# Two encoder layers on one core: grouped heads' output weights summed by accumulating transfers, and the second sequence's rows loaded as squares for VectorE to transpose

## The chip, the cores and the metric

The kernel runs on one core of a Trainium2 chip. Its engines work beside each other, each on its own queue of instructions: TensorE (PE, with its weight loads as PEld), VectorE (DVE), ScalarE (ACT), GpSimd (POOL) and SyncE (SP), which here only issues transfers. Sixteen DMA engines move the data. The metric is the device time of one execution in microseconds. Before the change it is 481.82 us, the median of three runs (481.68 to 482.26).

## The reference, cut to what matters

Two layers, each an attention and a feed-forward part, each followed by a sum with its input and a layer norm. Only the first attention and the first feed-forward part meet the change. x has 2 sequences of 512 rows of 512 numbers; all is float32.

```python
q = (x @ Wq.T + bq).reshape(b, s, 32, 128)
sig_q = elu(q) + 1
q_sel = sig_q[:, :, ::4, :]                      # 8 heads are used
num = einsum('bshd,hde->bshe', q_sel, M)
den = einsum('bshd,hd->bsh', q_sel, z)[..., None] + 1e-6
out_heads = repeat(num / den, 4, axis=2)         # each result serves 4 heads
x = layernorm(x + out_heads.reshape(b, s, 4096) @ Wo.T)
# feed-forward: gate and up products, values truncated to integers, down product
x = layernorm(x + ffn(x))
```

Since each of the eight results is repeated for a group of four heads, the four blocks of Wo that belong to a group can be summed first: the result times the sum of the blocks is the same as the sum of the four products.

## The kernel before, in words

**Order.** One function writes the whole program for all engines. A scheduler of the framework orders the instructions of TensorE, VectorE and ScalarE, by priorities and a model of times; GpSimd's order is as written, and SyncE's transfers go out in the order of the program. `tc.issue_after` ties an instruction behind another. Pools of tiles set what waits for what: a tile with a tag gets the next buffer of that tag, and its first writer waits until the readers of the buffer's earlier tile are done. All PSUM tiles come from one pool of eight (`ps`, line 66).

**First attention.** `load_x(0)` (line 74) loads the four row blocks of sequence 0, SyncE and ScalarE in turn. `transposed` (line 106) turns row blocks into `xt`, with the 512 columns on partitions in four groups `k`: 16 TensorE transposes into PSUM, then four copies, two by ScalarE and two by VectorE (line 119). `queries(b, xt, h)` (line 328) makes head `h`: four matmuls of 128x512, ScalarE's `e` and `r` (lines 340 and 342), VectorE's `q` (line 344). The first loop over the heads (line 432) works on sequence 0, the second (line 442) on sequence 1. After head 4 of sequence 0, `turn_memory` (line 347) transposes the eight blocks of M. After head 6, `transposed(xs[1], "a01")` (line 439) transposes sequence 1, whose rows were loaded behind wq (line 295).

**Output weights.** For each head, two transfers (line 306) bring the four blocks of Wo as two tiles of two blocks. `sum_weights` (line 355) adds them with two instructions, one of 128x1024 and one of 128x512, four heads on VectorE and four on GpSimd. `fold(h)` (line 363) multiplies the sum by M's block on TensorE, and ScalarE puts the product, less its last column, into `mw` (lines 367 and 368); the last column of `mw` is z, copied there by GpSimd (line 326). The folds stand behind heads 0, 2, 3, 5 and 6 of sequence 1.

**Checks.** Beside this, ScalarE and VectorE check whether the gate and up weights are ternary: `largest` over chunk 0 (line 450), `scales` (line 455), and from head 3 of sequence 1 three `check_up` (line 417) for each head. Their weights `gu` come by SyncE behind the blocks of Wo (line 310), then the small weights of the second layer (lines 312 to 320).

**Reading.** `read(b, t, between)` (line 370) runs eight matmuls `po` for each of eight row blocks; ScalarE and VectorE divide and add them to x, GpSimd adds the first three heads' part (lines 396 and 405).

**End of the first feed-forward part.** `f0_down(i)` (line 625) runs the down product of row block `i` (11 matmuls into `pd`), ScalarE scales it (`scaled`, line 610), block `i - 1` is truncated and subtracted from x with its statistics taken (`added`, line 616), and block `i - 2` is normalised (line 635), tied behind the statistics of the block after it. Before the last block's product, line 677 calls `transposed(xs[0], "a10")`, which the second layer's attention (`pqk`, line 778) needs.

Of the kernel before, what the change touches and what calls it, by code (L numbers as in the profile page):

```python
# [10 lines left out]
F32 = mybir.dt.float32  # L11
# [8 lines left out]
P = 128  # L20
# [7 lines left out]
LN_EPS = 1e-5  # L28
DEN_EPS = 1e-6
LAST = HID - 1  # L30
LENT = 3
TOP12 = -4096
BELOW_HALF = 0.5 - 2.0**-13
# [3 lines left out]
def kernel(  # L37
# [36 lines left out]
    def load_x(b):  # L74
        for t in range(NT):
            x = xp.tile([P, HID], F32, tag="x", name=f"x_{b}_{t}")
            eng = nc.scalar if b == 0 and t % 2 else nc.sync
            eng.dma_start(x, x_in[b, ts(t, P), :])
            xs[b].append(x)

    load_x(0)
    bq = const.tile([D, NH], F32, tag="bq", name="bq")
    z = const.tile([D, NH], F32, tag="z", name="z")

    ident = const.tile([P, P], F32, tag="ident", name="ident")
    make_identity(nc, ident)
    ln_eps = const.tile([P, 1], F32, tag="ln_eps", name="ln_eps")
# [4 lines left out]
    nc.vector.memset(den_eps, DEN_EPS)  # L92
    below_half = const.tile([P, 1], F32, tag="below_half", name="below_half")
    nc.vector.memset(below_half, -BELOW_HALF)
    ones = const.tile([P, P], F32, tag="ones", name="ones")
    nc.vector.memset(ones, 1.0)


    rise = psum("rise")
# [52 lines left out]
    def layernorm_apply(out, row, stats):  # L152
        mv, rstd = stats
        nc.vector.tensor_scalar(
            out, row, mv[:, 0:1], rstd, ALU.subtract, ALU.mult
        )
# [119 lines left out]
    def pair_tile(name):  # L276
        return wop.tile([P, 2, HID], F32, tag="wo", name=name)
# [6 lines left out]
    with tc.tile_pool(name="a0w", bufs=1) as a0w, tc.tile_pool(name="a0", bufs=2) as a0:  # L284
        wq = []
        for h in range(NH):
            if h % 2 == 0:
                two = query_tile(f"wq{h}").rearrange("p a (k d) -> p a k d", k=NK)
            w = two[:, h % 2]
            nc.sync.dma_start(w, wq_in[h])  # L290
            wq.append(w)
            if h == 0:
                nc.sync.dma_start(bq, bq_in)
                nc.sync.dma_start(z, z_in)
        load_x(1)
        m = a0w.tile([D, NH, D], F32, tag="m", name="m")
        nc.sync.dma_start(m, m_in)

        wos = []
        for h in range(NH):  # L300
            halves = []
            if h == 6:
                gus = up_weights(gu0_in, "0", range(1))
            for j in range(2):
                w = pair_tile(f"wo{h}_{j}")
                nc.sync.dma_start(w, wo0_in[h, :, ts(j, G // 2), :])
                halves.append(w)
            wos.append(halves)

        gus += up_weights(gu0_in, "0", range(1, len(CHUNKS)))  # L310
        wqkv = const.tile([P, NK, 3 * D], F32, tag="wqkv", name="wqkv")
        nc.sync.dma_start(wqkv, wqkv_in.rearrange("(k p) f -> p k f", p=P))
        bqk = const.tile([D, 3], F32, tag="bqk", name="bqk")
        nc.sync.dma_start(bqk, bqk_in)
        bv = const.tile([P, D], F32, tag="bv", name="bv")
        nc.sync.dma_start(bv, bv_in.to_broadcast([P, D]))
        wo1 = const.tile([D, HID], F32, tag="wo1", name="wo1")
        nc.sync.dma_start(wo1, wo1_in)
        bo = const.tile([P, HID], F32, tag="bo", name="bo")
        nc.sync.dma_start(bo, bo_in.to_broadcast([P, HID]))  # L320

        mw = a0w.tile([D, NH, HID], F32, tag="mw", name="mw")
        nc.gpsimd.tensor_copy(mw[:, :, LAST], z)

        def queries(b, xt, h, cuts=1):

# [25 lines left out]
        def sum_weights(eng, h):  # L355

            w, w1 = wos[h]
            eng.tensor_add(w, w, w1)
            s = a0.tile([D, HID], F32, tag="wos", name=f"wos{h}", bufs=4)
            eng.tensor_add(s, w[:, 0, :], w[:, 1, :])  # L360
            wos[h] = s

        def fold(h):
            p = psum(f"pmw_{h}")
            nc.tensor.matmul(p, m[:, h, :], wos[h], start=True, stop=True)
            c = small.tile([P, 1], F32, tag="col", name=f"col_{h}")
            nc.scalar.mul(c, p[:, LAST:], -1.0)
            nc.scalar.activation(mw[:, h, :LAST], p[:, :LAST], AF.Identity, bias=c)

        def read(b, t, between):  # L370

            x = xs[b][t]
            ys, steps = [], []
            for h0 in range(0, NH, 4):
                four = []
                den = small.tile([P, 4], F32, tag="den", name=f"den_{b}_{t}_{h0}")
                for j in range(4):
                    po = psum(f"po0_{b}_{t}_{h0 + j}")
                    nc.tensor.matmul(  # L379
                        po, qs[b][h0 + j][:, ts(t, P)], mw[:, h0 + j, :],  # L380
                        start=True, stop=True,
                    )
# [49 lines left out]
        for h in range(NH):  # L432
            queries(0, xt, h, 1 if h else 2)
            if h == 4:
                sum_weights(nc.gpsimd, 0)
                turn_memory()
                sum_weights(nc.vector, 1)
            elif h == 6:
                xt1 = transposed(xs[1], "a01")
                sum_weights(nc.vector, 2)  # L440
        sum_weights(nc.gpsimd, 3)
        for h in range(NH):
            queries(1, xt1, h)
            if h == 0:
                sum_weights(nc.vector, 4)
                sum_weights(nc.gpsimd, 5)
                fold(0)
                fold(1)
                mx_up = largest(
                    [gus[0][:, a].rearrange("p k i -> p (k i)") for a in range(2)], "up"  # L450
                )
            elif h == 1:
                top_up = over_partitions(mx_up, "up")
            elif h == 2:
                sc_up, inv_up = scales(top_up, "up")
                fold(2)
                fold(3)
                sum_weights(nc.vector, 6)
                sum_weights(nc.gpsimd, 7)
            elif h == 3:  # L460
                fold(4)
            elif h == 5:
                fold(5)
                fold(6)
            elif h == 6:
                fold(7)
            if h >= 3:
                for _ in range(3):
                    check_up(*checks.pop(0))
# [54 lines left out]
    with tc.tile_pool(name="f0", bufs=2) as f0:  # L524
# [88 lines left out]
            cut_to_12(y)  # L613
            ys[i] = y

        def added(i):
            b, t = order[i]
            ta, tb = truncated_parts(f0, ys[i], P, f"d{i}")

            x = xs[b][t]  # L620
            nc.vector.scalar_tensor_tensor(x, tb, 128.0, x, ALU.min, ALU.subtract)
            nc.vector.scalar_tensor_tensor(x, x, -1.0, ta, ALU.mult, ALU.add)
            stats[i] = layernorm_stats(x, f"f0_{i}")

        def f0_down(i):
            if i < len(order):
                pds[i] = down(*order[i])
                scaled(i)
            if 0 <= i - 1 < len(order):
                added(i - 1)  # L630
            if 0 <= i - 2 < len(order):

                b, t = order[i - 2]
                with tc.issue_after(taken[f"f0_{min(i, len(order)) - 1}"].ins):
                    layernorm_apply(xs[b][t], xs[b][t], stats[i - 2])

        to_divide[2:2] = [None, None]
        for c in range(3):
# [35 lines left out]
        up(1, 10, moved.values())  # L674
        for i in range(2, len(order) - 1):
            f0_down(i)
        xt_a1 = [transposed(xs[0], "a10")]
        for i in range(len(order) - 1, len(order) + 2):
            f0_down(i)

    gus = up_weights(gu1_in, "1", range(6, len(CHUNKS)))
# [487 lines left out]
```

## Time and profile before

| | |
|---|---|
| median of three runs | 481.82 us |
| the profiled execution's own time | 481.89 us |
| its span, first to last instruction | 479.7 us |
| granted TensorE clock, mean | 0.997 |
| data moved by transfers | 33.98 MB, 20.18 MB of it in the first 80 us |
| wo transfers (line 306) | 16 of 512 KB, median 7.6 us from issue to landing |
| transposes of sequence 1 (line 115) | 16, first weight load at 31.71 us |
| first fold, last fold (weight loads) | 40.33 us, 67.98 us |
| first matmul of the read stage (weight load) | 71.85 us |
| first pqk of the second layer | 239.17 us |

The span counts from the first to the last instruction of the profiled execution; some 2.2 us lie around it. In lines of the timeline the first number is the start in microseconds, the second the length; "xN" counts merged instructions, and the brackets at the end give the idle time of the engine before and what released it. float32 matmuls of 128x512 stand in the profile as two instructions, 0.43 us apart.

### The profile page before, as it was taken

The page shows a single profiled execution, that of the slowest core. Times are in us where ns is not written, and L with a number is a line of the kernel's source. Part 1 is how long each engine was busy: PE and PEld are TensorE (multiplying, and loading weights), DVE is VectorE, ACT ScalarE, POOL GpSimd, SP SyncE. Part 2 cuts the span into 40 slices and gives each one's busy share as a digit, 9 for nine tenths or more (in the row PEclk, how much of TensorE's full clock was granted, in tenths as well). Part 3 has the DMA queues.
Part 4 walks back from the last instruction along what each step waited for, and adds up shares of the span by engine and source line. Part 5 has one row for each costly group of instructions (what it writes and reads, how often), then busy time and mean ns, then how long its engine had stood idle before and what let it go on. Part 6 is the DMA issues. An engine that isn't in the chain of part 4 may idle for free.

```text
span 479.7 us, 5815 instructions
## 1 busy us (share of the span) xinstructions
PE 470.9 (98%) x1891; PEld 329.6 (69%) x1891; DVE 349.9 (73%) x689; ACT 272.5 (57%) x512; POOL 115.1 (24%) x146
## 2 busy tenths in 40 slices
PE   9999999999999999999999999999999999999995
PEld 8454444434487788787766567888788888888885
DVE  1345677677666586756979989997875778999852
ACT  3344899556666867546645834686753565434221
POOL 0344102666530392000464032000000000023211
PEclk9999999999999999999999999999999999999998
DMA  8999700000043001121390000000000000001011
GB/s 303 389 357 336 296 2 0 0 0 1 2 128 110 3 1 26 65 91 34 113 385 2 0 1 1 1 1 0 1 0 1 1 1 1 0 23 40 27 45 44
DMA packets 13748, 33.98 MB, mean 71 GB/s; under 512 B 1872, under 2 KB 2768, under 8 KB 13712
## 3 DMA queue, kind: packets, MB, share of 16 engines
q1 hardware_dynamic: 13280, 32.85, 19.0%
q10 hardware_dynamic: 432, 0.66, 0.4%
q8 instruction: 22, 0.36, 0.3%
q14 instruction: 14, 0.11, 0.1%
HBM read 31.40 MB, written 2.10 MB: 70 GB/s over the span
## 4 chain that ended last, share of the span: by engine, by line
PE 71%; ACT 7%; DVE 5%; issue 3%; POOL 1%; POOLq 0%; DVEq 0%; ACTq 0%
PE pm L977 17%; PE pg_f L539 9%; PE pc L977 9%; PE pu_f L539 9%; PE pdm L1052 7%; PE pd_f L595 4%; PE pdc L1052 4%; DVE x L401 4%; PE pqk L778 3%; PE po L379 2%; ACT y L392 2%; ACT t L411 2%; PE pv L791 1%; PE po L880 1%; PE pot L863 1%
## 5 line engine op out<-in xcount | busy, mean ns | idle before, releaser
L379 PE MATMUL po<-mw,q 128*128 128x512 f32 x128 | 57.1, 598 | 0.4 <-DVE mv_a L142 0.2
L334 PE MATMUL pq<-xt_a,wq 128*128 128x512 f32 (+1 forms) x136 | 56.4, 567 | 0.0
L148 POOL TENSOR_TENSOR rstd_f<-mv_f,ln_eps 128x1 f32<-128x1 f32 x15 | 4.7, 313 | 185.8 <-DVE mv_f L1063 132.1
L379 PEld LDWEIGHTS po<-mw,q 128*128 128x128 f32 x128 | 23.0, 189 | 32.2 <-issue 17.7
L334 PEld LDWEIGHTS pq<-xt_a,wq 128*128 128x128 f32 x136 | 25.5, 190 | 27.5 <-issue 25.5
L977 PE MATMUL pm<-r,it_early 128*128 128x512 f32 x144 | 37.8, 393 | 0.4 <-ACT r L718 0.4
L977 PE MATMUL pm<-r,ugu 128*128 128x512 f32 (+1 forms) x144 | 36.8, 393 | 0.0
L977 PEld LDWEIGHTS pm<-r,it_early 128*128 128x128 f32 x144 | 27.0, 188 | 6.7 <-ACT r L718 0.7
L401 DVE SCALAR_TENSOR_TENSOR x<-po,den,x 128x511 f32<-128x511 f32 x40 | 29.8, 745 | 1.9
L977 PEld LDWEIGHTS pm<-r,ugu 128*128 128x128 f32 (+1 forms) x144 | 26.8, 186 | 6.3
L170 ACT ACTIVATE ta_f<-y_f,below_half 128x512 int8<-128x512 f32 (+1 forms) x22 | 15.9, 722 | 24.4 <-DVE y_f L160 23.9
L988 DVE SCALAR_TENSOR_TENSOR ev_q<-pm,ev_q 128x512 f32<-128x512 f32 (+1 forms) x28 | 19.2, 687 | 14.0 <-PE pm L977 14.0
L396 POOL TENSOR_TENSOR y<-y,y 128x511 f32<-128x511 f32 x16 | 20.3, 1270 | 31.5 <-ACT y L392 30.8
L565 DVE SCALAR_TENSOR_TENSOR it_f<-tb_f,ta_f 128x512 fp32r<-128x512 int16 (+1 forms) x22 | 15.2, 690 | 16.0 <-ACT tb_f L171 15.9
L977 PE MATMUL pc<-r,ugu 128*128 128x512 f32 (+1 forms) x96 | 26.1, 394 | 0.0
L340 ACT ACTIVATE e<-pq,bq 128x512 f32<-128x512 f32 x16 | 11.1, 693 | 25.8 <-PE pq L334 25.8
L413 POOL TENSOR_SCALAR td<-wd,inv_down 128x512 fp32r<-128x512 f32 (+1 forms) x11 | 19.5, 1792 | 24.8 <-DVE inv_down L204 24.4
L539 PE MATMUL pg_f<-xh,tu 128*128 128x512 f32 (+1 forms) x88 | 25.1, 405 | 0.0
L539 PE MATMUL pu_f<-xh,tu 128*128 128x512 f32 (+1 forms) x88 | 24.0, 394 | 0.0
L539 PE MATMUL pg_f<-xl,tu 128*128 128x512 f32 (+1 forms) x88 | 23.9, 393 | 0.0
L539 PE MATMUL pu_f<-xl,tu 128*128 128x512 f32 (+1 forms) x88 | 23.9, 393 | 0.0
L987 ACT ACTIVATE ev_q<-pc 128x512 f32<-128x512 f32 (+1 forms) x28 | 16.4, 591 | 12.1 <-PE pc L977 12.1
(292 smaller groups left out, 1106.0 us busy)
## 6 DMA issues: line engine op xcount, KB each, us to landing
gu<-in_gu SPq DMA_DIRECT2D x20, 512.0 KB, 7.9
wo<-in_wo SPq DMA_DIRECT2D x16, 512.0 KB, 7.6
wd<-in_wd SPq DMA_DIRECT2D x20, 256.0 KB, 4.7
wq<-in_wq SPq DMA_DIRECT2D x8, 256.0 KB, 4.5
out<-x SPq DMA_DIRECT2D x7, 256.0 KB, 2.0
x<-in_x SPq DMA_DIRECT2D x6, 256.0 KB, 5.4
gu<-in_gu SPq DMA_DIRECT2D x2, 384.0 KB, 6.5
wqkv<-in_wqkv SPq DMA_DIRECT2D x1, 768.0 KB, 10.8
```

Of the source, the lines that this page charges most:

```text
L170: nc.scalar.activation(a[:n], y, AF.Relu, bias=below_half[:n])
L334: nc.tensor.matmul(pq[:, at], wq[h][:, k, :], xt[:, k, at], start=(k == 0), stop=(k == NK - 1),)
L379: nc.tensor.matmul(po, qs[b][h0 + j][:, ts(t, P)], mw[:, h0 + j, :], start=True, stop=True,)
L396: nc.gpsimd.tensor_add(ys[0][:, :LAST], ys[0][:, :LAST], y[:, :LAST])
L401: steps.append(nc.vector.scalar_tensor_tensor(x[:, :LAST], four[j][:, :LAST], d, x[:, :LAST], ALU.mult, ALU.add))
L413: eng.tensor_scalar(out, w, factor, None, ALU.mult)
L539: nc.tensor.matmul(pp[a][:n], t[:, a, i % NK, :n], x2[b][i], start=(i == 0), stop=(i == 2 * NK - 1),)
L595: nc.tensor.matmul(pd, inter[b][c][:n, ts(t, P)], td[c][:n].bitcast(F32R), start=(c == 0), stop=(c == last),)
L977: nc.tensor.matmul(p[:n], w, x, start=(left[id(p)] == begun[id(p)]), stop=(left[id(p)] == 1))
L987: nc.scalar.activation(ev[:n], pc, AF.Copy, scale=CROSS)
L988: nc.vector.scalar_tensor_tensor(ev[:n], pm, MAIN, ev[:n], ALU.mult, ALU.add)
L1052: nc.tensor.matmul(p[:, :w], got[j // 4][1][kind][:n, j % 4], down_parts[j][kind][:, cols], start=(j == 0 and kind == kinds[0]), stop=(j = ...
```

## The change

It has three parts.

First, the sums of Wo's blocks. `sum_weights` goes. Four tiles `wos[i]` hold a pair of heads each. SyncE loads block 0 of both heads into each (four transfers of 512 KB in pieces of 2 KB); then GpSimd issues twelve transfers with `accum_op=ALU.add`, blocks 1, 2 and 3 of each pair in turn, which add to what is in the tile. `fold` reads the tile directly. The folds move: two behind each of heads 4 to 7 of sequence 1.

Second, sequence 1's rows. They are first loaded as `x_squares`, in the buffer that later holds `mw`: 16 transfers of 64 KB, each with 32 partitions and pieces of 32 numbers (128 B), so that each 32x32 square of x lies where its transpose belongs. Four VectorE transposes of 128x512, which turn each 32x32 square in place, then give `xt1`. `mw` is taken after this (`begin_fold`), its column of z is loaded straight by SyncE, in pieces of one number, and behind it in SyncE's order come the rows of sequence 1 themselves (`load_x(1)`, needed in the read stage), chunks 1 to 10 of `gu`, and the second layer's small weights (`others`).

Third, smaller moves. The constant `ones` is set first. At the end of the first feed-forward part the last down product is issued ahead of the 16 transposes of `transposed(xs[0], "a10")`; the truncation of block 6 is tied behind ScalarE's two copies; the normalisation of the last block of a sequence is tied behind the second subtraction of the next block (`taken[n]`) in place of its statistics.

```diff
-            if h == 0:
-                nc.sync.dma_start(bq, bq_in)
-                nc.sync.dma_start(z, z_in)
-        load_x(1)
+        wos = [pair_tile(f"wo{i}") for i in range(NH // 2)]
+
+        def load_wo(eng, i, g, **how):
+            pair = wo0_in[ts(i, 2), :, g, :].rearrange("h d e -> d h e")
+            eng.dma_start(wos[i], pair, **how)
+
+        x_squares = a0w.tile([P, NK, S], F32, tag="mw", name="x_squares")
+        squares = x_in[1].rearrange("(f i) (k a j) -> k a i f j", i=SQ, k=NK, j=SQ)
         m = a0w.tile([D, NH, D], F32, tag="m", name="m")
         nc.sync.dma_start(m, m_in)
-        wos = []
-        for h in range(NH):
-            halves = []
-            if h == 6:
-                gus = up_weights(gu0_in, "0", range(1))
-            for j in range(2):
-                w = pair_tile(f"wo{h}_{j}")
-                nc.sync.dma_start(w, wo0_in[h, :, ts(j, G // 2), :])
-                halves.append(w)
-            wos.append(halves)
-        gus += up_weights(gu0_in, "0", range(1, len(CHUNKS)))
+        for k in range(NK):
+            for a in range(P // SQ):
+                nc.sync.dma_start(
+                    x_squares[ts(a, SQ), k].rearrange("i (f j) -> i f j", j=SQ),
+                    squares[k, a],
+                )
+        for i in range(NH // 2):
+            load_wo(nc.sync, i, 0)
+        for g in range(1, G):
+            for i in range(NH // 2):
+                load_wo(nc.gpsimd, i, g, accum_op=ALU.add)
+        gus = up_weights(gu0_in, "0", range(1))
...
+        def begin_fold():
+            mw = a0w.tile([D, NH, HID], F32, tag="mw", name="mw")
+
+            nc.sync.dma_start(mw[:, :, LAST], z_in)
+            mws.append(mw)
...
             elif h == 6:
-                xt1 = transposed(xs[1], "a01")
-                sum_weights(nc.vector, 2)
-        sum_weights(nc.gpsimd, 3)
+                xt1 = xtp.tile([P, NK, S], F32, tag="xt", name="xt_a01")
+                for k in range(NK):
+                    nc.vector.transpose(xt1[:, k, :], x_squares[:, k, :])
+                begin_fold()
+                load_x(1)
+                gus += up_weights(gu0_in, "0", range(1, len(CHUNKS)))
+                others()
...
+            elif h >= 4:
+                fold(2 * h - 8)
+                fold(2 * h - 7)
...
+        def normed(i):
+
+            b, t = order[i]
+            n = min(i + 1, len(order) - 1)
+
+            with tc.issue_after(taken[n if t == NT - 1 else f"f0_{n}"].ins):
+                layernorm_apply(xs[b][t], xs[b][t], stats[i])
...
+        i = len(order) - 1
+        pds[i] = down(*order[i])
+        scaled(i)
         xt_a1 = [transposed(xs[0], "a10")]
-        for i in range(len(order) - 1, len(order) + 2):
+        added(i - 1, (copies[-4], copies[-2]))
+        normed(i - 2)
+        for i in range(len(order), len(order) + 2):
             f0_down(i)
```

More of the change, by code (lines that the diff above doesn't have):

```diff
@@ L30 @@
 LAST = HID - 1
+SQ = 32
 LENT = 3
@@ L82 @@
     bq = const.tile([D, NH], F32, tag="bq", name="bq")
-    z = const.tile([D, NH], F32, tag="z", name="z")
+    ones = const.tile([P, P], F32, tag="ones", name="ones")
+    nc.vector.memset(ones, 1.0)
     ident = const.tile([P, P], F32, tag="ident", name="ident")
@@ L94 @@
     nc.vector.memset(below_half, -BELOW_HALF)
-    ones = const.tile([P, P], F32, tag="ones", name="ones")
-    nc.vector.memset(ones, 1.0)
     rise = psum("rise")
@@ L311 @@
+        for i in range(NH // 2):
[4 more added lines that the diff above has]
+        gus = up_weights(gu0_in, "0", range(1))
         wqkv = const.tile([P, NK, 3 * D], F32, tag="wqkv", name="wqkv")
-        nc.sync.dma_start(wqkv, wqkv_in.rearrange("(k p) f -> p k f", p=P))
         bqk = const.tile([D, 3], F32, tag="bqk", name="bqk")
-        nc.sync.dma_start(bqk, bqk_in)
@@ L315, with others @@
         bv = const.tile([P, D], F32, tag="bv", name="bv")
-        nc.sync.dma_start(bv, bv_in.to_broadcast([P, D]))
         wo1 = const.tile([D, HID], F32, tag="wo1", name="wo1")
-        nc.sync.dma_start(wo1, wo1_in)
         bo = const.tile([P, HID], F32, tag="bo", name="bo")
-        nc.sync.dma_start(bo, bo_in.to_broadcast([P, HID]))
-        mw = a0w.tile([D, NH, HID], F32, tag="mw", name="mw")
-        nc.gpsimd.tensor_copy(mw[:, :, LAST], z)
+        def others():
+            nc.sync.dma_start(wqkv, wqkv_in.rearrange("(k p) f -> p k f", p=P))
+            nc.sync.dma_start(bqk, bqk_in)
+            nc.sync.dma_start(bv, bv_in.to_broadcast([P, D]))
+            nc.sync.dma_start(wo1, wo1_in)
+            nc.sync.dma_start(bo, bo_in.to_broadcast([P, HID]))
@@ L328, in queries @@
+        mws = []
+        def begin_fold():
+            mw = a0w.tile([D, NH, HID], F32, tag="mw", name="mw")
+            nc.sync.dma_start(mw[:, :, LAST], z_in)
+            mws.append(mw)
         def queries(b, xt, h, cuts=1):
@@ L353, in turn_memory @@
                 nc.scalar.copy(m[:, 4 * i : 4 * i + 4, :].rearrange("d h e -> d (h e)"), pt)
[L355 to L361, printed above, removed]
         def fold(h):
             p = psum(f"pmw_{h}")
-            nc.tensor.matmul(p, m[:, h, :], wos[h], start=True, stop=True)
+            nc.tensor.matmul(p, m[:, h, :], wos[h // 2][:, h % 2, :], start=True, stop=True)
             c = small.tile([P, 1], F32, tag="col", name=f"col_{h}")
             nc.scalar.mul(c, p[:, LAST:], -1.0)
-            nc.scalar.activation(mw[:, h, :LAST], p[:, :LAST], AF.Identity, bias=c)
+            nc.scalar.activation(mws[0][:, h, :LAST], p[:, :LAST], AF.Identity, bias=c)
         def read(b, t, between):
@@ L379, in read @@
                     nc.tensor.matmul(
-                        po, qs[b][h0 + j][:, ts(t, P)], mw[:, h0 + j, :],
+                        po, qs[b][h0 + j][:, ts(t, P)], mws[0][:, h0 + j, :],
                         start=True, stop=True,
@@ L434 @@
             if h == 4:
-                sum_weights(nc.gpsimd, 0)
                 turn_memory()
-                sum_weights(nc.vector, 1)
             elif h == 6:
-                xt1 = transposed(xs[1], "a01")
-                sum_weights(nc.vector, 2)
-        sum_weights(nc.gpsimd, 3)
+                xt1 = xtp.tile([P, NK, S], F32, tag="xt", name="xt_a01")
[5 more added lines that the diff above has]
+                others()
         for h in range(NH):
@@ L444 @@
             if h == 0:
[L445 to L448, printed above, removed]
                 mx_up = largest(
@@ L455 @@
                 sc_up, inv_up = scales(top_up, "up")
[L456 to L466, printed above, removed]
+            elif h >= 4:
+                fold(2 * h - 8)
+                fold(2 * h - 7)
             if h >= 3:
@@ L614, in scaled, with added @@
             ys[i] = y
-        def added(i):
+        def added(i, behind=()):
             b, t = order[i]
-            ta, tb = truncated_parts(f0, ys[i], P, f"d{i}")
+            with ExitStack() as tied:
+                for step in behind:
+                    tied.enter_context(tc.issue_after(step.ins))
+                ta, tb = truncated_parts(f0, ys[i], P, f"d{i}")
             x = xs[b][t]
             nc.vector.scalar_tensor_tensor(x, tb, 128.0, x, ALU.min, ALU.subtract)
-            nc.vector.scalar_tensor_tensor(x, x, -1.0, ta, ALU.mult, ALU.add)
+            taken[i] = nc.vector.scalar_tensor_tensor(x, x, -1.0, ta, ALU.mult, ALU.add)
             stats[i] = layernorm_stats(x, f"f0_{i}")
@@ L631, in f0_down @@
             if 0 <= i - 2 < len(order):
-                b, t = order[i - 2]
-                with tc.issue_after(taken[f"f0_{min(i, len(order)) - 1}"].ins):
-                    layernorm_apply(xs[b][t], xs[b][t], stats[i - 2])
+                normed(i - 2)
[4 more added lines that the diff above has]
+                layernorm_apply(xs[b][t], xs[b][t], stats[i])
         to_divide[2:2] = [None, None]
@@ L676 @@
             f0_down(i)
+        i = len(order) - 1
+        pds[i] = down(*order[i])
+        scaled(i)
         xt_a1 = [transposed(xs[0], "a10")]
-        for i in range(len(order) - 1, len(order) + 2):
+        added(i - 1, (copies[-4], copies[-2]))
+        normed(i - 2)
+        for i in range(len(order), len(order) + 2):
             f0_down(i)
```

## The prediction

> **What bounds the kernel now.** I began with the page's first parts: the span, the busy shares, and the forty slices with what the DMA engines moved.
>
> ```profile
> span 479.7 us, 5815 instructions
> PE 470.9 (98%) x1891; PEld 329.6 (69%) x1891; DVE 349.9 (73%) x689; ACT 272.5 (57%) x512; POOL 115.1 (24%) x146
> PE   9999999999999999999999999999999999999995
> DMA  8999700000043001121390000000000000001011
> PE 71%; ACT 7%; DVE 5%; issue 3%; POOL 1%; POOLq 0%; DVEq 0%; ACTq 0%
> ```
>
> TensorE (PE) is busy throughout, and the chain of waits runs through it for 71% of the span. So a TensorE instruction removed is worth its spacing, and a wait put before TensorE costs its length. But the first five slices (60 us) are also full of DMA, so transfers there are not free. The view of windows gives that stage: length, then busy time of PE, PEld, DVE, ACT and POOL, granted clock, DMA share, GB/s.
>
> ```profile
> 12.00:32.00 20.00, 20.00 (x54) 9.28 (x53) 8.99 (x11) 7.43 (x13) 7.53 (x4) 1.00 1.00 368
> 32.00:53.00 21.00, 21.00 (x64) 10.17 (x63) 10.25 (x19) 10.78 (x22) 7.12 (x4) 1.00 0.95 365
> 53.00:72.00 19.00, 19.00 (x46) 8.48 (x45) 14.10 (x33) 18.45 (x36) 0.44 (x1) 1.00 0.23 80
> 72.00:131.00 59.00, 58.65 (x149) 25.10 (x147) 42.44 (x96) 39.59 (x107) 31.06 (x33) 1.00 0.00 1
> 233.00:240.00 7.00, 5.96 (x32) 4.49 (x31) 6.82 (x16) 4.85 (x9) 2.61 (x6) 1.00 0.64 202
> ```
>
> The reader is to see full DMA engines until 53 us, ACT full from 53 to 72, no transfers from 72 to 131, and a gap of TensorE at 233 to 240. Then I took the timeline of TensorE's weight loads around the second sequence's transposes and folds, and of the gap.
>
> ```profile
> 31.29 0.19 PEld L334 LDWEIGHTS pq<-xt_a,wq 128*128 128x128 f32 x1 [0.24 <-issue]
> 31.71 0.14 PEld L115 LDWEIGHTS pt_a<-ident,x 128*128 128x128 f32 x1 [0.24 <-issue]
> 33.78 0.30 PEld L334 LDWEIGHTS pq<-xt_a,wq 128*128 128x128 f32 x2
> 37.89 0.49 PEld L334 LDWEIGHTS pq<-xt_a,wq 128*128 128x128 f32 x2 [0.37 <-DVE xt_a L119]
> ...
> 236.88 0.53 DVE L154 TENSOR_SCALAR x<-x,mv_f,rstd_f 128x512 f32<-128x512 f32 x1
> 238.55 1.06 ACT L119 COPY xt_a<-pt_a 128x512 f32<-128x512 f32 x2
> 239.17 4.13 PE L778 MATMUL pqk<-xt_a,wqkv 128*128 128x512 f32 x9 [1.04 <-ACT xt_a L119]
> ```
>
> Ordinary loads start 0.43 us apart. Last, the DMA view of a tenth of a microsecond in which bq and z arrive, for the price of a small packet.
>
> ```profile
> DMA packets 121, 0.03 MB, mean 256 GB/s; under 512 B 110, under 2 KB 110, under 8 KB 121
> q1 hardware_dynamic: 121, 0.03, 119.4%
> ```
>
> **What the skill says.** Trainium skill, "Collectives: The Full Stack", section "The bandwidth ceiling": an add inside a DMA needs two source reads for each write, and runs at about half the rate of a copy (62.28 against 32.35 GB/s there). No transfer of the kernel before accumulates. "DMA: Bandwidth & Descriptors", "Issuing engines are not separate DMA queues": transfers issued by GpSimd and by SyncE share the same 16 DMA engines and interleave. The trace shows one busy queue only, and cannot say how two share. Same page, "Why small descriptors are slow (HBM only)": each packet carries a fixed overhead. The trace agrees mildly: the 11 big packets above take some 85 ns each (2 KB at 24 GB/s per engine, 16 engines at about 380 GB/s), 0.94 of the 1.91 us of engine time (119.4% of 0.1 us on 16 engines), which leaves 8.8 ns for each of the 110 small ones. "VectorE: DVE Perf Modes", "The three transpose paths": VectorE transposes blocks of 32x32 only, which the squares supply; no VectorE transpose stands in the trace.
>
> **The change, part by part.**
>
> *Transposes of the second sequence leave TensorE.* From 31.29 to 33.78 are 2.49 us between two loads that would stand 0.43 apart: 2.06. The wait for the copy at 37.89 costs 0.37 - 0.24 = 0.13. Together -2.2. Two copies each leave ACT and VectorE; neither was full there.
>
> *Four VectorE transposes come.* I take the 0.68 us of its 128x512 copies, bounded by half and by double: 2.7 us (1.4 to 5.4). VectorE is busy 9 of 20 us from 12 to 32, and loses more than it gains: eight sums (four of 1.22, four of 0.69, 7.6 us). Cost 0. In the compiled order the first stands behind q of head 0, the last behind q of head 5, so a late square holds q, then ACT's e, whose buffers run out; TensorE has the eight tiles of the PSUM pool as cover. The last runs at about 31 us (head 5's matmuls end at 7.2 + 6x3.43 + 0.87 = 28.7, then e, r, q). TensorE needs the rows at 7.2 + 8x3.43 + 0.87 = 35.5.
>
> *Squares.* 16 DMAs of 512 pieces of 128 B: 512 per engine. At 8.8 ns plus 3.5 for the 96 further bytes, 6.3 us; lower bound the 2.6 us that 1 MB takes at 400 GB/s, upper three times mine, 19. They follow x, wq and m (3.5 MB, landed at about 11), so they land at 18 to 20; an issue costs SyncE 0.33 to 0.43 us, 16 take about 6 us beside the data. The first sums of wo (2 MB) follow and land from 22 to 26.
>
> *Accumulating transfers.* Twelve of 512 KB from GpSimd, each behind the one before it on its pair. On GpSimd nothing useful queues behind them until y at 79 us, and its own four sums (14.9 us) go. The price c of one in engine time: at least the 1.3 us of a plain 512 KB at 400 GB/s, at most 2.6 with the double read. The first fold now stands behind head 4. Before, that head ended at 58.97; without five folds (5x0.86) and 2.2, 52.5. Pair 0's third transfer is the ninth. Until 31 us the twelve are nearly alone; then VectorE's last transpose frees the buffer of mw, for which SyncE's load of z waits, and behind z come 1 MB of rows, ten gu and the small weights, 7.6 MB, 19 us at 400 GB/s. If both queues share evenly, a transfer takes 2c from there: the ninth ends at 31.5 + (9 - 9.5/c) x 2c + 2 (latency) = 14.5 + 18c. That is 37.9 at c = 1.3 and 52.3 at c = 2.1: no stall up to there. I take c = 2 or less in effect, since the added read is from SBUF and a GpSimd packet may win more than half; cost 0. At c = 2.6 the ninth ends at 61.3, a stall of 8.8; the other pairs follow 5.2 us apart, as fast as TensorE asks (3.43 + 2x0.86 = 5.15).
>
> *Folds at heads 4 to 7.* ACT per head, by its spacings: e and r 0.57 each, three t and a tu 0.61 each, two col and mw 0.65 each: 4.9 us against TensorE's 5.15. It fits; if not, ACT's backlog grows by 0.7 us a fold. The eight folds cost TensorE the same as before.
>
> *z later, ones earlier.* SyncE loses 0.43 us at the start; TensorE's first transposes wait for x until 4.52. Nothing. z as 1,024 elements is far from its use.
>
> *The gap at 233.* The last down product goes ahead of all 16 transposes, row 3's normalisation moves ahead of one statistics and one subtraction on VectorE (0.69 each, from 236.88 to about 235.5), and ACT's two copies go ahead of the truncations. The products end at about 236.2, 16 transposes of 0.107 end at 237.9, a copy at 238.6: pqk starts 0.5 earlier than 239.17, and loses less later (7.13 for 6.87). -0.6, bounds 0 and -1.0.
>
> **Sum.** -2.2 - 0.6 = -2.8 against the profiled execution's 481.9 (span 479.7 and 2.2 around it), which stands at the median of 481.82: **479.1 us**.
>
> **Rivals.** *Late sums* (slower): the one mechanism is the accumulation's engine time, at the first fold; it decides from c above 2.1. At c = 2.6, 479.1 + 8.8 = 488; from 483 to 491 as sharing goes. For it: the page's factor of two and 368 GB/s already before the change. Against: the transfers have 9 us alone, and at c = 2 the whole of 24 + 19 + 1 us from 22 on ends at 66, before the last folds at 52.5 + 3x5.15 = 68. *Slow squares* (slower): at 19 us the sums start 12 us later, all in contention: 34 + 18c + 2 is 59 at c = 1.3 and 74 at 2.1, stalls of 7 and 21: 486 to 500. For it: packets of 128 B from HBM, never tried here at length. Against: the small packets' 8.8 ns. *Absorbed* (no change): TensorE reaches the read stage 2.2 us earlier, but there the chain of waits runs through ACT and VectorE and TensorE then waits for them: 481.9 - 0.6 = 481.3. Against: TensorE lost only some 2 us in those 59, and ACT's backlog also begins 2.2 + 4x0.86 = 5.6 us earlier (four folds no longer stand ahead of the factors for the checks). That the transfers don't run beside each other at all would show as late sums.
>
> **How the numbers follow.** Forecast 0.48, late sums 0.28, slow squares 0.12, absorbed or a small stall 0.12. 0.2% (1 us) is about what a measurement of this kernel can tell. Faster takes the forecast and a quarter of the last: 0.51; same 0.09; slower, the two rivals: 0.40. The likeliest one's own range is 478.3 to 480.8. To leave out no more than 2 in 10 the range goes to 490: outside stay most of slow squares (0.09), the end of late sums (0.05), a forecast too small (0.04).
>
> **What would show it.** Right: no pt_a transposes at 32; weight loads of pq 0.43 apart from head 7 to the first fold; the first pmw near 52.5 with no wait on a DMA; the read stage starting at about 69.7; pqk at 0.5 us less after the last pd than before. Wrong: an idle TensorE before pmw released by a DMA of wo (late sums), or before pq of sequence 1 released by VectorE's transposes (slow squares); issue times of several microseconds on GpSimd.

## The result, and the profile after

The changed kernel takes 487.65 us (median of four runs, 487.53 to 490.45) where the kernel before, now with a fourth run, takes 481.88 us: a ratio of 1.0133, with a 95% interval of 1.0096 to 1.0169. It is slower by 1.3%, clear of the noise. Its profiled execution took 487.76 us, 485.5 of it span, so the two spans differ by 5.8 us.

First the page of the changed kernel: its span, busy time, and three rows of its forty slices (12.1 us each), then the shares of the chain of waits.

```profile
span 485.5 us, 5798 instructions
...
PE 470.6 (97%) x1875; PEld 329.2 (68%) x1875; DVE 341.7 (70%) x683; ACT 272.0 (56%) x510; POOL 114.1 (24%) x149
...
PE   9999499999999999999999999999999999999995
...
PEclk9999879999999999999999999999999999999999
DMA  8999994000006000312192000000000000000011
...
PE 84%; DMA 10%; issue 2%; SPq 2%; DVE 1%; POOL 0%; ACT 0%; POOLq 0%
```

TensorE's row has one hole, the fifth slice (48.6 to 60.7 us), and the clock's row a dip behind it. The chain of waits, which had no DMA share worth a figure before, now has 10%. The DMA engines stay full through the fifth slice and are at 4 tenths in the sixth (before: 7 tenths and nothing). The view of windows has the same columns as in the prediction:

```profile
12.00:32.00 20.00, 20.00 (x53) 9.19 (x53) 6.21 (x10) 7.52 (x13) 5.79 (x5) 1.00 1.00 228
32.00:53.00 21.00, 21.00 (x51) 8.90 (x49) 7.00 (x15) 7.94 (x13) 7.65 (x7) 1.00 1.16 233
53.00:72.00 19.00, 12.08 (x22) 5.23 (x22) 9.12 (x22) 13.56 (x26) 1.20 (x1) 0.73 1.08 308
72.00:131.00 59.00, 59.00 (x152) 27.06 (x151) 39.42 (x92) 43.09 (x113) 27.83 (x29) 1.00 0.11 38
```

Read the last two numbers of the second row: the DMA engines are at least as busy as before (1.16 against 0.95), but move 233 GB/s in place of 365. In the third row TensorE works 12.08 of 19 us, at a mean clock of 0.73. Now the weight loads of TensorE around the first fold, the first fold's matmul itself, and the gap at the end of the first feed-forward part (start, length; in the brackets the idle time before):

```profile
52.03 0.19 PEld L350 LDWEIGHTS pq<-xt_a,wq 128*128 128x128 f32 x1 [0.24 <-issue]
59.93 0.50 PEld L373 LDWEIGHTS pmw<-wo,m 128*128 128x128 f32 x2 [7.71 <-ACT t L419]
59.96 2.90 PE L373 MATMUL pmw<-wo,m 128*128 128x512 f32 x3 [6.92 <-DMA wo<-in_wo]
60.95 0.34 PEld L373 LDWEIGHTS pmw<-wo,m 128*128 128x128 f32 x1 [0.52 <-ACT tu L419]
61.80 0.34 PEld L373 LDWEIGHTS pmw<-wo,m 128*128 128x128 f32 x1 [0.52 <-issue]
...
66.07 0.23 PEld L350 LDWEIGHTS pq<-xt_a,wq 128*128 128x128 f32 x1 [0.52 <-issue]
66.54 0.19 PEld L350 LDWEIGHTS pq<-xt_a,wq 128*128 128x128 f32 x1 [0.24 <-issue]
...
241.88 0.54 DVE L154 TENSOR_SCALAR x<-x,mv_f,rstd_f 128x512 f32<-128x512 f32 x1
...
244.13 1.07 ACT L119 COPY xt_a<-pt_a 128x512 f32<-128x512 f32 x2 [0.67 <-PE pt_a L115]
...
244.77 1.99 PE L789 MATMUL pqk<-xt_a,wqkv 128*128 128x512 f32 x4 [0.35 <-ACT xt_a L119]
```

TensorE could have loaded the first fold's weights at 52.46 and did so at 59.93: 7.5 us late. Then its loads stand 0.85 us apart in place of 0.43 until 66.5. The fold waits for a transfer. The brackets name ScalarE's `t` for the weight load, but `t` is no operand of a fold; the matmul's own line (59.96) names the transfer, `<-DMA wo<-in_wo`. (A wait for several things is put down to the one that came last by the profile.) GpSimd's queue shows the transfers. Each issue of blocks 2 and 3 waits until the transfer before on the same pair has landed, so from the fifth issue on (31.25) an issue's start is the landing of the transfer four places ahead:

```profile
23.52 5.23 POOL L300 DMA_DIRECT2D wo<-in_wo  x4 [22.22 <-DMA wo<-in_wo]
31.25 1.19 POOL L300 DMA_DIRECT2D wo<-in_wo  x1 [2.50 <-DMA wo<-in_wo]
34.48 1.19 POOL L300 DMA_DIRECT2D wo<-in_wo  x1 [2.03 <-DMA wo<-in_wo]
37.06 1.20 POOL L300 DMA_DIRECT2D wo<-in_wo  x1 [1.39 <-DMA wo<-in_wo]
39.67 1.20 POOL L300 DMA_DIRECT2D wo<-in_wo  x1 [1.41 <-DMA wo<-in_wo]
42.23 1.20 POOL L300 DMA_DIRECT2D wo<-in_wo  x1 [1.36 <-DMA wo<-in_wo]
45.61 1.20 POOL L300 DMA_DIRECT2D wo<-in_wo  x1 [2.18 <-DMA wo<-in_wo]
50.02 1.20 POOL L300 DMA_DIRECT2D wo<-in_wo  x1 [3.21 <-DMA wo<-in_wo]
55.08 1.20 POOL L300 DMA_DIRECT2D wo<-in_wo  x1 [3.85 <-DMA wo<-in_wo]
```

The first lands at 31.25, the second 3.2 us behind it. Up to 42 the next follow 2.6 us apart, then 3.4, 4.4 and 5.1. The eighth lands at 55.08, and the ninth, which completes pair 0, at about 59.8. The account of the spans, by where each stage of TensorE begins (before, after):

| stage begins | before | after | gained or lost since the line above |
|---|---|---|---|
| first pq | 7.10 | 6.54 | -0.6 |
| first po (read stage) | 71.85 | 79.84 | +8.6 |
| first pg_f (feed-forward) | 130.62 | 137.12 | -1.5 |
| first pqk (second layer) | 239.17 | 244.77 | -0.9 |
| end of span | 479.7 | 485.5 | +0.2 |

### The profile page after: what moved, and what is told of

It reads as the page before. It is cut to its first block, busy times and chain, and to the rows that moved or that the text cites. A ratio compares the mean times of both kernels' runs of the same rounds, so it can differ in the third digit from the quotient of the medians.

```text
span 485.5 us, 5798 instructions
## 1 busy us (share of the span) xinstructions
PE 470.6 (97%) x1875; PEld 329.2 (68%) x1875; DVE 341.7 (70%) x683; ACT 272.0 (56%) x510; POOL 114.1 (24%) x149
## 3 DMA queue, kind: packets, MB, share of 16 engines
q1 hardware_dynamic: 21408, 27.61, 17.5%
## 4 chain that ended last, share of the span: by engine, by line
PE 84%; DMA 10%; issue 2%; SPq 2%; DVE 1%; POOL 0%; ACT 0%; POOLq 0%
PE pm L988 17%; PE po L387 11%; PE pg_f L537 9%; PE pc L988 8%; PE pu_f L537 8%; DMA wo<-in_wo 8%; PE pdm L1063 7%; PE pd_f L593 4%; PE pdc L1063 4%; PE pqk L789 3%; PE pq L350 2%; PE pmw L373 2%; SPq L309 2%; PE pv L802 1%; PE po L891 1%
## 5 line engine op out<-in xcount | busy, mean ns | idle before, releaser
L350 PE MATMUL pq<-xt_a,wq 128*128 128x512 f32 (+1 forms) x136 | 57.6, 579 | 0.0
L387 PE MATMUL po<-mw,q 128*128 128x512 f32 x128 | 55.9, 594 | 0.1
L988 PEld LDWEIGHTS pm<-r,it_early 128*128 128x128 f32 x144 | 26.9, 188 | 6.6 <-ACT r L729 0.7
L360 DVE SCALAR_TENSOR_TENSOR q<-e,r 128x512 f32<-128x512 f32 x16 | 11.0, 690 | 27.6 <-ACT r L358 27.6
L209 DVE SCALAR_TENSOR_TENSOR junk<-t,sc_up,gu 128x512 int8<-128x512 f32 (+1 forms) x22 | 16.3, 739 | 13.6 <-ACT t L419 13.0
L421 POOL TENSOR_SCALAR td<-wd,inv_down 128x512 fp32r<-128x512 f32 (+1 forms) x11 | 19.5, 1792 | 24.8 <-DVE inv_down L204 24.4
L300 POOL DMA_DIRECT2D wo<-in_wo x12 | 14.6, 1225 | 40.3 <-DMA wo<-in_wo 40.2
```

The costliest lines, as they stand in the source:

```text
L209: nc.vector.scalar_tensor_tensor(junk, t, sc, w, ALU.mult, ALU.not_equal, accum_out=count)
L350: nc.tensor.matmul(pq[:, at], wq[h][:, k, :], xt[:, k, at], start=(k == 0), stop=(k == NK - 1),)
L387: nc.tensor.matmul(po, qs[b][h0 + j][:, ts(t, P)], mws[0][:, h0 + j, :], start=True, stop=True,)
L421: eng.tensor_scalar(out, w, factor, None, ALU.mult)
L988: nc.tensor.matmul(p[:n], w, x, start=(left[id(p)] == begun[id(p)]), stop=(left[id(p)] == 1))
```

## The experiments

My theory after the result: the loss is the rival called late sums, an add inside the transfer that costs the DMA engines twice a copy and is then shared with other loads. Against it stood: the squares or VectorE's transposes cost something of their own; GpSimd's way of issuing is the slow part; the halved clock has a cause of its own. Times are medians; the ratio is against the kernel before, with its 95% interval.

| run | us | ratio |
|---|---|---|
| e1_sums_on_engines | 488.06 | 1.012 (1.0101 to 1.0139) |
| e2_accumulates_only | 490.83 | 1.0178 (1.0159 to 1.0198) |
| e3_tail_only | 480.76 | 0.9974 (0.9963 to 0.9984) |
| e4_kept_warm | 488.61 | 1.013 (1.0106 to 1.0154) |
| e4b_kept_warm_longer | 487.31 | 1.011 (1.0094 to 1.0126) |
| e5_no_gu_loads | 482.52 | 1.0009 (0.9992 to 1.0025) |
| e6_no_add | 477.78 | 0.9929 (0.991 to 0.9947) |
| e7_squares_engine_sums | 486.49 | 1.0101 (1.0086 to 1.0116) |
| e8_two_of_three_adds | 482.69 | 1.0019 (1.0008 to 1.003) |
| e9_adds_not_held | 483.65 | 1.0038 (1.0026 to 1.0049) |
| e10_changed_again | 488.60 | 1.0146 (1.0127 to 1.0166) |
| e11_no_accumulates | 482.92 | 1.0023 (1.0017 to 1.003) |

### The add taken out of the transfers

```diff
-                load_wo(nc.gpsimd, i, g, accum_op=ALU.add)
+                load_wo(nc.gpsimd, i, g)
```

> The changed kernel with the twelve transfers of GpSimd in the same order and behind the same waits, but without the add: each overwrites the tile (the sum of Wo's blocks is left out). If the add itself costs a second pass: alone they go 1.3 to 1.6 us apart in place of 2.6, the ninth lands before 45 us, no wait at the first fold, 477.5. If GpSimd's issue (1.2 us each) or the chain of landings sets the pace: spacing stays 2.6 and more, and 486 to 488.

It took 477.78 us, 9.9 less than the changed kernel, where 10.2 (7.5 of waiting and 2.7 of halved clock) were at stake. GpSimd's queue, the weight loads of the folds (the last two times are the first and last start), and the window from 32 to 53 us:

```profile
31.69 0.72 POOL L300 DMA_DIRECT2D wo<-in_wo  x1 [1.86 <-DMA wo<-in_wo]
33.09 0.72 POOL L300 DMA_DIRECT2D wo<-in_wo  x1 [0.67 <-DMA wo<-in_wo]
34.40 0.72 POOL L300 DMA_DIRECT2D wo<-in_wo  x1 [0.59 <-DMA wo<-in_wo]
35.73 0.72 POOL L300 DMA_DIRECT2D wo<-in_wo  x1 [0.60 <-DMA wo<-in_wo]
```

```profile
L373 PEld LDWEIGHTS pmw<-wo,m x16: 190/190/190, 52.5 to 69.3; 128*128 128x128 f32 x16
```

```profile
32.00:53.00 21.00, 21.00 (x52) 9.14 (x51) 9.56 (x21) 11.90 (x20) 5.49 (x8) 1.00 1.03 371
```

The same transfers from the same engine behind the same waits land 1.3 to 1.4 us apart in place of 2.6 (up to 36 us; beside the rows and gu, from 39.7 on, 2.0 to 2.6 in place of up to 5.1), the DMA engines move 371 GB/s in place of 233, the first fold starts at 52.5 and the read stage at 69.7, where the prediction had them. So the add makes them slow. The chain of landings is the same in both. An issue is shorter without the add (0.72 against 1.20 us), but even 1.20 is less than half of the spacing of 2.6, and the DMA engines are full (the DMA view below), so issuing doesn't set the pace. The squares, VectorE's transposes and the late folds bring no wait of TensorE for data here.

The packets differ too. From 30 to 31 us GpSimd's queue has the engines to itself in both kernels: with the add it moves 110 packets of some 1.9 KB (207 GB/s), without it 101 of some 3.6 KB (365 GB/s). Small pieces alone don't explain the half rate, since SyncE's plain packets of some 2 KB moved at 418 GB/s in the changed kernel just before (25 to 26 us). A packet with the add takes about as long as a plain one of twice its size.

### The competing loads taken out

```diff
+            nc.gpsimd.memset(gu.rearrange("p a k i -> p (a k i)"), 0.0)
...
-                gus += up_weights(gu0_in, "0", range(1, len(CHUNKS)))
+                gus += zeros
```

> The changed kernel with chunks 1 to 10 of gu set to zero by GpSimd early on instead of loaded (that part of the gate and up weights is left out), so that 5.1 MB do not share the DMA engines with the sums. If the sums are late because they share: spacing of the accumulating transfers stays at 2.6 us, the ninth lands near 49 us, TensorE does not wait at the first fold near 52.5, no halved clock, 487.65 - 10.2 = 477.5. If an accumulating transfer is that slow by itself: the ninth still near 58 to 60 us and 486 to 488. In either case the spacing gives the price of one alone.

482.52 us lies between the two. GpSimd's queue in this run:

```profile
37.61 1.20 POOL L300 DMA_DIRECT2D wo<-in_wo  x1 [1.41 <-DMA wo<-in_wo]
40.15 1.20 POOL L300 DMA_DIRECT2D wo<-in_wo  x1 [1.35 <-DMA wo<-in_wo]
42.78 1.20 POOL L300 DMA_DIRECT2D wo<-in_wo  x1 [1.43 <-DMA wo<-in_wo]
46.18 1.20 POOL L300 DMA_DIRECT2D wo<-in_wo  x1 [2.19 <-DMA wo<-in_wo]
49.94 1.20 POOL L300 DMA_DIRECT2D wo<-in_wo  x1 [2.56 <-DMA wo<-in_wo]
53.73 1.20 POOL L300 DMA_DIRECT2D wo<-in_wo  x1 [2.59 <-DMA wo<-in_wo]
```

The spacing is 2.6 until 42.8 and then 3.4 to 3.8, from the rows and small weights that are still loaded; the first fold starts at 56.9 with a wait of 3.7. So the loads of gu account for 3 of the 7.5 us. At 2.6 throughout, the ninth would land eight spacings behind the first, at about 52 (31.25 + 20.8) in the changed kernel: price and sharing are both needed for the wait.

How two queues share shows in the DMA view: packets, MB and share of the 16 engines for GpSimd's queue (q0) and SyncE's (q1). In the changed kernel, first from 32 to 42 us, then from 45 to 60:

```profile
q0 software_dynamic: 1021, 1.96, 107.0%
q1 hardware_dynamic: 901, 0.10, 13.1%
```

```profile
q0 software_dynamic: 905, 1.74, 62.4%
q1 hardware_dynamic: 909, 2.52, 46.8%
```

The counts are near one to one in both, once GpSimd's packets have begun to move. While SyncE's next packets are z's single numbers, its 901 packets bring 0.10 MB and hardly delay the sums; once they are pieces of rows and gu, each packet of a sum waits for a big one, and a sum takes 5.05 us in place of 2.6. The kernel with the sums alone, below, has 1467 to 1462 packets from 24 to 50 us. That the engines take one packet from each queue in turn, whatever its size, is what these counts suggest; it was not tested otherwise.

### One part alone

```diff
+        for g in range(1, G):
+            for i in range(NH // 2):
+                load_wo(nc.gpsimd, i, g, accum_op=ALU.add)
...
+            elif h >= 4:
+                fold(2 * h - 8)
+                fold(2 * h - 7)
```

> The kernel before with the accumulating transfers and the later folds alone: TensorE transposes, rows of sequence 1 loaded early, gu right behind the first sums. TensorE would reach the first fold near 54.7 us. Late sums: a wait there for a transfer of wo; the twelve start near 18 us and share from the start, so at some 4.2 us each the ninth lands near 57, a wait of 2 to 3 us, and up to 2.7 more if the clock falls again: 484 to 488. If the loss needs the squares or the late loads behind z: no wait, 481.9 or less.

490.83 us, slower than expected. GpSimd's queue, then the first fold's weight load:

```profile
28.59 1.19 POOL L303 DMA_DIRECT2D wo<-in_wo  x1 [5.86 <-DMA wo<-in_wo]
34.18 1.19 POOL L303 DMA_DIRECT2D wo<-in_wo  x1 [4.39 <-DMA wo<-in_wo]
39.26 1.20 POOL L303 DMA_DIRECT2D wo<-in_wo  x1 [3.89 <-DMA wo<-in_wo]
```

```profile
63.14 0.50 PEld L358 LDWEIGHTS pmw<-wo,m 128*128 128x128 f32 x2 [8.42 <-issue]
```

Here gu stands right behind the first sums, so sharing begins at once: the first landings follow 5.0 to 5.6 us apart. From 49 us on, when what is left to load has smaller packets, they follow 2.9 to 3.7 apart, and the mean spacing of the first eight landings (4.4) is near the 4.2 that I had taken. What I had not taken is the start: the first sum, issued at 17.5, lands only at 28.6. The wait is 8.2 us longer than an ordinary 0.24, and the fold's matmul again names a transfer of wo. The first part of the change brings the loss without the other two.

The third part alone, the order at the end of the first feed-forward part:

```diff
+        i = len(order) - 1
+        pds[i] = down(*order[i])
+        scaled(i)
         xt_a1 = [transposed(xs[0], "a10")]
+        added(i - 1, (copies[-4], copies[-2]))
+        normed(i - 2)
```

> The kernel before with the third part alone: last down product ahead of the transposes, the tied truncation and normalisation. The two traces compared give 0.9 us for that stage: 481.0. If that 0.9 belongs to something else that differs between the two kernels: 481.7 to 482.

480.76 us. In its trace pqk starts 107.6 us behind the first pg_f (131.2 to 238.8), 108.55 before: the 0.9 us belong to this part. It is the only complete version here that beats both kernels.

### The clock behind the wait

```diff
+                with tc.issue_after(last_pq[0].ins):
+                    for _ in range(10):
+                        step = nc.tensor.matmul(warm, ones, qs[0][0], start=True, stop=True)
```

The first of the two runs had eight matmuls; ScalarE's checks were tied to the old order in both.

> The changed kernel with eight more matmuls of 128x512 on TensorE, whose product nobody reads, behind head 4 of sequence 1 and ahead of the first fold: 8 x 0.86 = 6.9 us, inside the 7.5 us in which TensorE waits for the sums. If the halved clock after the wait comes from the idle time: no weight loads 0.85 us apart after 60 us, and 487.65 - 2.7 = 485.0. If it comes from elsewhere (the transfers, the time of the run): 487.5, loads 0.85 apart for 6.6 us.

> As e4_kept_warm with ten matmuls (8.6 us), which should end near 61 us and leave TensorE less than 1.5 us of waiting. If idle time alone halves the clock: no weight loads 0.85 us apart, the read stage starts 2 to 3 us sooner than without the ten for the same landing of the sums, 485 to 486. If not: loads 0.85 apart for 3 us or more, 487 to 488.5.

> The changed kernel itself once more, for a second profile: if the landing of the ninth transfer moves from execution to execution, the first fold starts somewhere between 59.9 and 63 us here too, as in the two runs with added matmuls, which then can't be compared by their times alone; if it is at 59.9 again, the added matmuls themselves made the sums later. Time 487 to 489.

The times, 488.61 and 487.31 us, show no gain, and decide nothing: the ninth sum landed later in both executions. Its fold starts at 62.02 with eight and 62.60 with ten, against 59.93 and 60.53 in the two of the changed kernel; all of that lateness is there at the seventh landing, 51.94 and 52.69 against 50.02 and 50.63, and the added matmuls begin only at 52.7, so they did not make it. The stretch from there to the read stage doesn't depend on the landing. It is 19.9 us in the changed kernel (59.93 to 79.84), 19.5 in its second profile (60.53 to 80.0), 16.8 with ten matmuls (62.60 to 79.4), 17.2 without the add. The weight loads of the run with ten, those 0.24 behind the one before left out:

```profile
62.60 0.30 PEld L384 LDWEIGHTS pmw<-wo,m 128*128 128x128 f32 x2 [1.98 <-ACT r L360]
63.99 0.19 PEld L352 LDWEIGHTS pq<-xt_a,wq 128*128 128x128 f32 x1 [0.24 <-ACT col L386]
```

No load stands 0.85 us apart there. With eight matmuls TensorE waited 3.1 us and its loads were 0.85 apart for some 3.5 us. So the halved clock follows the idle time, and keeping TensorE busy takes it away. Trainium skill, "TensorE: Matmul & The Clock Gate", section "HAM oscillation — how this bites in real kernels", says that gaps of more than about 3.4 us without work halve the clock. These traces agree on the effect and show no sharp limit. By the idle times in the brackets there is half speed after 3.1, 7.7 and 8.4 us, and after 3.7 in the run without gu, there only from 1.4 us behind the wait on; full speed after 2.0 and, in the run e9 below, after 4.2.

### Other ways to make the sums

Two attempts to keep the squares and sum on the engines as before:

```diff
+            summed[h] = eng.tensor_add(s, w[:, 0, :], w[:, 1, :])
...
+            nc.gpsimd.tensor_copy(mw[:, :, LAST], z)
```

> The changed kernel with its squares, its VectorE transposes and its tail, but Wo's blocks loaded plainly and summed by VectorE and GpSimd as before, with the folds at their old places. Late sums (all of the loss lies in the accumulating transfers): 481.9 less 2.2 for the transposes and 0.9 for the gap at the end of the first feed-forward part, 478.8, between 478.3 and 479.5; first read matmul near 69.6 us. If the squares or the VectorE transposes cost something of their own: 482 or more, with TensorE waiting before sequence 1's first head. If the gain before the read stage is absorbed there: near 481.

> As e1_sums_on_engines, with its two own faults mended: squares go ahead of all of Wo again, GpSimd copies z after its last sum and not between them, and VectorE's sums of heads 1, 2 and 4 are tied ahead of q of heads 4, 6 and 7. Late sums: no wait longer than 1 us before the read stage, first read matmul near 69.6 us, 478.3 to 479.5. If the squares cost something of their own (5 us more of transfers ahead of gu): ScalarE or TensorE waits for gu, 481 or more.

Both missed, at 488.06 and 486.49, and neither for the reason under test: no fold waits for a sum. In the first I had put GpSimd's copy of z between its sums. It waits for the buffer of the squares, so that sums, their buffers and the loads behind them (gu among them) stood still. (The brackets name a transfer of wo; but the copy starts as VectorE's last transpose of the squares ends, 37.63 + 0.70 = 38.33.) GpSimd's queue, then TensorE:

```profile
38.40 0.20 POOL L341 COPY mw<-z 128x8 f32<-128x8 f32 x1 [19.08 <-DMA wo<-in_wo]
```

```profile
50.27 0.08 PEld L190 LDWEIGHTS pmx_up<-ident,mx_up 128*2 128x2 f32 x1 [6.83 <-issue]
```

In the second, with the ties that I put on VectorE, the scheduler set `e` of head 6 behind the first fold on ScalarE:

```profile
37.86 0.17 ACT L386 ACTIVATE col<-pmw 128x1 f32<-128x1 f32 x1 [8.17 <-PE pmw L384]
```

They say nothing of the price of the squares; the run without the add does. Then three attempts at a complete faster version, with the folds late: four of the twelve adds on VectorE, the same with nothing held up, and no accumulating transfer at all.

```diff
+                    added_up.append(nc.vector.tensor_add(wos[i], wos[i], seconds[i]))
+                for g in range(2, G):
...
+                        load_wo(nc.gpsimd, i, g, accum_op=ALU.add)
```

> The changed kernel with eight accumulating transfers in place of twelve: the second blocks of each pair are loaded plainly into tiles of their own (the pool has two left) and added by VectorE, four adds of 128x1024; only the third and fourth blocks accumulate, and q of heads 5, 6 and 7 is tied behind these adds. Pair 0 is then complete after the fifth accumulating transfer in place of the ninth, at 2.6 to 5 us each from about 29 us on: 42 to 50 us, ahead of the first fold at 52.5; the eighth by 66, ahead of the last folds at 68. Late sums: no wait at the folds, no halved clock, read stage from 69.7 us, the time of the changed kernel without the add: 477.3 to 478.5. If any accumulating transfer in this stage costs TensorE time by another way (contention with the other transfers or with the engines' own accesses): above 480.

> As e8_two_of_three_adds, with what held it there taken away: two more tiles so that no plain load waits for an add, the accumulating transfers ordered by the folds' need (pair 0 twice among the first three), and the rows of sequence 1 behind gu. Late sums: e8's two waits of 2.6 and 2.7 us go, read stage from about 69.7 us, 477.0 to 478.5, under the kernel before and the tail alone (480.8). If the transfers are short of bandwidth as a whole: a wait on wo or gu stays, 480 or more.

```diff
+                        nc.sync.dma_start(w, pair)
+                        nc.gpsimd.tensor_add(wos[i], wos[i], w)
```

> The changed kernel with squares, tail and the late folds, but no accumulating transfer: blocks 1 to 3 of each pair are loaded plainly into four tiles in turn; VectorE adds block 1, GpSimd blocks 2 and 3 with eight adds of 128x1024 (2.34 us each as in the kernel before, from about 31 to 52 us; pair 0 complete near 43); the rows of sequence 1 go behind gu. Late sums (the accumulating transfers are the one thing that costs): no wait at the folds, read stage from 69.7 us, 477.3 to 479, below the kernel before and the tail alone (480.8). If the squares' slow transfers (8 us for 1 MB) push gu or Wo out too far: a wait for gu or wo, 480 to 483.

All three are 4 to 5 us faster than the changed kernel, but slightly slower than the kernel before, and none reaches 478. In e8 the last plain load lands only at 40 us among the accumulating transfers; VectorE waits for it, then TensorE for ScalarE (2.6 us), and the first fold waits 2.7. In e9 the first fold is in time (52.4), but the later folds wait 1.8, 4.2 and 1.7 us for wo. That is the other reading of its expectation: the DMA engines are full from 24 to 70 us (a share of 1.02 to 1.17). My order adds to it: it puts two transfers of a pair close together, with little in flight between them, so that GpSimd's queue moves 6 packets from 40 to 42 us and none from 67.5 to 68.6. How much each costs was not separated. In e11 no fold waits, yet VectorE is held up. Its queue, at instructions that take 0.69 us alone:

```profile
33.94 0.69 DVE L367 SCALAR_TENSOR_TENSOR q<-e,r 128x512 f32<-128x512 f32 x1 [0.47 <-ACT r L362]
...
37.37 2.79 DVE L367 SCALAR_TENSOR_TENSOR q<-e,r 128x512 f32<-128x512 f32 x1 [1.58 <-ACT r L362]
40.81 2.10 DVE L367 SCALAR_TENSOR_TENSOR q<-e,r 128x512 f32<-128x512 f32 x1 [0.65 <-ACT r L362]
```

GpSimd's eight adds run from 37.26 to 58.5. Through them TensorE waits 2.1 us at pmx_up, and the checks, done late, lengthen the read stage to 60.2 us (72.0 to 132.2).

## Why the prediction was wrong

*Transposes off TensorE, -2.2; folds unchanged.* Right in kind; that the numbers fit is luck. TensorE was ready for the first fold at 52.46 (52.5 forecast), and without the add the read stage starts at 69.7, the forecast number. But that includes an earlier first pq (0.5 us there); from first pq to the read stage it is 64.75 us before and 63.1 without the add, so 1.65 of the 2.2. The lines had been misread: the two loads at 33.78 start 0.11 apart, not 0.43, and the next one stands at 34.32. From 31.29 to 34.32 are 3.03 us for three spacings of 0.43, so the transposes cost 1.74 and not 2.06. The 0.13 at 37.89 was made up in the same way. The last 0.1 went to pmx_up, around which three spacings take 1.50 us in place of 1.40.

*Squares and VectorE's transposes, cost 0.* Right. A transpose took 0.705 us (0.68 taken). The first one ran at 14.87, the last at 30.25; no matmul of sequence 1 waited for them. (VectorE's own sums cost more than the 7.6 us taken: one of the four of 128x1024 took 2.27 us before, not 1.22, so the room was larger.) The 1 MB of squares moved from about 11 to 19.5 us, some 8 us in which the DMA engines were at first full and then at 73 to 88% (6.3 taken). The rival slow squares did not happen.

*Accumulating transfers, cost 0: the step that failed.* The working had the right formula and bounds, 1.3 to 2.6, and then "I take c = 2 or less in effect, since the added read is from SBUF and a GpSimd packet may win more than half". The measured c is 2.6 us without big packets beside it, the upper bound, which was the price of the Trainium skill's factor of two; shared, it is up to 5.05 in the changed kernel, so a GpSimd packet wins no more than its turn. For a c below the bound the working gave these two reasons and no measurement. With c = 2.6 the working gave 61.3 for the landing and 488 for the time; measured, about 59.8 and 487.65. The stall was 7.5 us (8.8).

*Inside that formula two errors offset each other.* The first 9.5 us were not free for the sums: three more plain transfers of wo and gu's first chunk, issued earlier, were still arriving, and by 31.25 one sum had landed in place of 3.7. GpSimd issued from 23.52 on, but its first packet moved at 26.9, and SyncE's queue had the engines until then; in the run with the sums alone the issue was at 17.5 and the first packet at 22.3, with gu arriving all the while. Whether the delay is GpSimd's own or comes from packets already in line was not separated; the working had no such term. On the other side sharing began only at 42, not 31.5, since z's single numbers stood at the head of SyncE's queue.

*Not foreseen: the clock.* The halved clock behind the stall cost 2.7 us (19.9 against 17.2 us from the first fold to the read stage). The late-sums case had no such term. That its 488 is so near to 487.65 is luck: the stall was 1.3 us shorter than in that sum, and the read stage, below, 1.5 us shorter.

*The gap at 233, -0.6.* Right in kind, 0.9 in size: the copies were ready, and pqk's wait fell from 1.04 to 0.35.

*The read stage: absorbed or not.* Not absorbed. It became 1.5 us shorter, also without the stall (57.4 us in the run without the add, 58.8 before). In the trace of before TensorE's idle time there behind ScalarE's den and y was 10.4 us, after it was 2.9. Which reordering on ScalarE did it is not settled. Nor is the 0.6 us at the start, which lies within what first pq shows between executions of these versions (6.4 to 7.5 us).

In sum: -0.6 at the start, -1.65, -1.5 and -0.9 against 7.5, 2.7 and 0.2 at the end give +5.8, the difference of the spans.

## What to carry to other kernels

An add moved into transfers is not free work: here it took the DMA engines twice a plain copy's time, and in a stage whose DMA engines are full already it delays everything queued beside it, itself most. Before moving work onto DMA, count engine time up to the deadline of the first reader, with the other queue's packets interleaved, and where the Trainium skill gives a factor of two take it unless something measured says less. If a stall does come, price its aftermath too: after 7.5 us of waiting TensorE worked another 6.6 us at half speed.

## What the runs showed of the hardware that I had not expected

- GpSimd spends 1.20 us on issuing a 512 KB transfer with the add, 0.72 us on the same one without.
- GpSimd's first packet moved 2.5 to 4.8 us behind the start of its issue, each time with SyncE's queue filling the engines: 3.4 in the changed kernel, 4.8 with the sums alone, 2.5 without the add.
- Small packets shield the other queue. In the changed kernel z, 1,024 single numbers in a transfer of 4 KB, took 14.5 us from issue to landing, and the rows and gu behind it crept along (0.10 MB in 10 us), while the sums kept their 2.6 us.
- Beside GpSimd's adds of 128x1024 (e11) VectorE's q took between 1.4 and 2.8 us in place of 0.69. Trainium skill, "GPSIMD Engine Reference", section "1. Specifications", says that GpSimd shares its SBUF interfaces with VectorE, with contention for instructions that read two inputs from SBUF. q reads two, and e11 agrees. The trace of before had shown it once: VectorE's sum of 2.27 us began while GpSimd's of 128x512 ran.
